# A tuned two-layer graph-attention kernel: first rows on two queues, right weights loaded earlier, scaling, residual rows and bias work moved

## The chip, the cores and the metric

One core of one Trainium2 chip. The metric is the device time of one execution in microseconds (us), as the median of several runs.

The engines in the traces: PE is TensorE, DVE is VectorE, ACT is ScalarE, POOL is GpSimd, SP is SyncE. SPq and ACTq are the points where SyncE and ScalarE issue transfers. SBUF is the on-chip memory that holds tiles, PSUM the banks into which TensorE writes. X, Y, Z and V are four of these banks, and the products are named after them. An evacuation is the step of VectorE or ScalarE that reads a finished bank and so frees it. The granted clock is the share of TensorE's full clock that the trace records: 0.50 is half rate.

## The reference

128 graphs of 64 nodes with 768 features, float32. Two layers of attention between layer norms, the weights 768x768:

```python
h = maximum(layernorm(x), 0)
for l in range(2):
    m_left, m_right = h @ W_left[l].T, h @ W_right[l].T
    u_left  = einsum('bih,bjh->bij', h, m_left)  / sqrt(768)
    u_right = einsum('bih,bjh->bij', h, m_right) / sqrt(768)
    u = upper triangle with diagonal from u_left, the rest from u_right (with adj)
    e = exp(u) * adj
    att = e / (sum(e) + 1e-10)
    ctx = att @ (h @ W_lin[l].T + b_lin[l])
    h = relu(layer_norm(ctx, ln_a[l], ln_b[l]))
return x + h
```

## The kernel before

It works on 16 blocks of 512 rows. Each layer has two passes: the first projects each block with the left and right weights and makes the attention; the second makes the linear product, the context and the norm. Each product of a 768x768 weight uses a scheme of seven half-size products instead of eight, which needs four sums of weight quarters (`sums_w`) and four sums of token quarters (`sums_t`). These sums read their inputs from SBUF.

```python
def sums_w(l, kind, eng):            # four sums, 128x1152 each
    ...
    for o, f, a, b in (("S1", "tensor_add", "S3", "A22"), ("S2", "tensor_sub", "S1", "A11"), ...):
        queue.append(lambda ...: getattr(eng, f)(t[o], t[a], t[b]))

def sums_t(key, eng=nc.gpsimd):      # four sums, 128x768 each: T1, T2, T3, T4
    ...
    for o, m, n in (("T1", "B12", "B11"), ("T2", "B22", "T1"), ("T3", "B22", "B12"), ("T4", "B21", "T2")):
        queue.append(lambda ...: sub(o, m, n))
```

Work beside the matmuls is put in a queue, and one piece is taken from it after each product (`pump(1)`). The order of the program is the order on each engine; nothing is rescheduled. The start of the first pass:

```python
if (l, 0) not in XR:
    load_rows(l, 0, sp)                    # rows of block 0, by SyncE
load_adj(0)
if l == 0:
    load_w(0, "l")
    transpose_rows(0, 0, sp)               # layer norm of the rows, transposes, store of the block
    flush()
    sums_t((1, 0, 0), nc.vector)           # on VectorE for this block alone
    ...
    sums_w(0, "l", nc.vector)
    ...
    load_w(0, "r")                         # issued behind the store
    sums_w(0, "r", nc.gpsimd)
queue.append(lambda: masks(0))
flush()
load_rows(l, 1, sp)
```

After this start, each block's queue holds the next block's preparation, and ends with `masks(u)` (GpSimd, needs the adjacency) and `sums_t` (GpSimd, needs the block). The third and fourth token sum are held back to the last product groups (`late`). In the second block, the last weights' bias work, centring and sums are appended, ahead of `late`.

Of the kernel before, what the change touches and what calls it, by code (L numbers as in the profile page):

```python
# [10 lines left out]
F32 = mybir.dt.float32  # L11
# [6 lines left out]
def kernel(  # L18
# [103 lines left out]
             ("X", "A12", "B21"), ("Z", "S4", "B22"), ("V", "A22", "T4"))  # L122

    HT, TS = {}, {}

    def tokens_of(key):
        ht = HT[key]
# [30 lines left out]
    nc.gpsimd.memset(eps_in, EPS_IN)  # L158
    floor = const.tile([P, 1], F32, name="floor")
    nc.gpsimd.memset(floor, 1e-30)  # L160

    diff = const.tile([P, S], I32, name="diff")
    tri = const.tile([P, 2, S], F32, name="tri")
# [2 lines left out]
        nc.gpsimd.iota(diff[r], pattern=[[-1, S]], base=0, channel_multiplier=1)  # L166
    nc.vector.tensor_scalar(tri[:, 0, :], diff, 0.0, None, op0=ALU.is_le)
    nc.vector.tensor_scalar(tri[:, 1, :], diff, 0.0, None, op0=ALU.is_gt)
    a_col, b_col = column("a_col", ln_a[0]), column("b_col", ln_b[0])

    def mean_var(mv, halves):
        st = stat.tile([P, 2, 6], F32, name="st")
        for n in range(2):
# [3 lines left out]

    XR = {}

    def load_rows(l, u, pool):  # L180

        XR[l, u] = []
        for g in range(2):
            t = pool.tile([P, 2, H], F32, name="x", bufs=2)
            for a in range(4):
                i = 4 * g + a
                src = x[u * NBB + i] if l == 0 else ROWS[u][i]
                nc.sync.dma_start(t[a * 32:(a + 1) * 32], src.rearrange("(k j) h -> j k h", k=2))
            XR[l, u].extend([t[:, 0, :], t[:, 1, :]])

    def load_h(which, l, u):
# [3 lines left out]
    def affine(which, l, u, step=1):  # L195

        def part(c0):
            for c in range(c0, c0 + step):
                ht = HT[which, l, u][:, c, :]
                nc.scalar.activation(ht, ht, AF.Relu, bias=b_col[:, c:c + 1], scale=a_col[:, c:c + 1])  # L200

        for c in range(0, C if l else 0, step):
            queue.append(lambda c=c: part(c))

    def transpose_rows(l, u, pool):

        key, xr = (1, l, u), XR[l, u]
        if l == 0:
            mv = stat.tile([P, Q, 2], F32, name="mv0", bufs=2)
            sd = stat.tile([P, Q], F32, name="sd0", bufs=2)  # L210
            rs = stat.tile([P, Q], F32, name="rs0", bufs=2)
            nb = stat.tile([P, Q], F32, name="nb0", bufs=2)

            def scale(q0, q1):
                nc.scalar.activation(sd[:, q0:q1], mv[:, q0:q1, 1], AF.Sqrt, bias=eps_in)
                nc.vector.reciprocal(rs[:, q0:q1], sd[:, q0:q1])
                nc.vector.scalar_tensor_tensor(nb[:, q0:q1], mv[:, q0:q1, 0], -1.0, rs[:, q0:q1],
                                               op0=ALU.mult, op1=ALU.mult)

            def norm(q):  # L220
                nc.scalar.activation(xr[q], xr[q], AF.Relu, bias=nb[:, q:q + 1], scale=rs[:, q:q + 1])

            for q in range(Q):
                queue.append(lambda q=q: mean_var(mv[:, q, :], [xr[q][:, :HH], xr[q][:, HH:]]))
                if u == 0:
                    queue.append(lambda q=q: scale(q, q + 1))
                    queue.append(lambda q=q: norm(q))
            if u:
                queue.append(lambda: scale(0, Q))
                for q in range(Q):  # L230
                    queue.append(lambda q=q: norm(q))
        if (l, u) == (0, 0):

            ht = HT[key] = big.tile([P, C, T], F32, name="ht")

            def turn(c0):
                p = ps_aux.tile([P, 2, T], F32, name="aux")
                for c in range(2):
                    for q in range(Q):
                        nc.tensor.transpose(p[:, c, q * P:(q + 1) * P],  # L240
                                            xr[q][:, (c0 + c) * P:(c0 + c + 1) * P], ident)
                for c in range(2):
                    nc.scalar.copy(ht[:, c0 + c, :].rearrange("p (a q j) -> p q a j", a=4, q=Q),
                                   p[:, c].rearrange("p (q a j) -> p q a j", a=4, q=Q))

            for c in range(0, C, 2):
                queue.append(lambda c=c: turn(c))
            queue.append(lambda: nc.sync.dma_start(KEPT[l][u], ht))
            return

        xb = pool.tile([P, H // 32, Q, 32], F32, name="xb", bufs=1)

        def store():
            to = KEPT[l][u].rearrange("(b i) c t -> i c b t", b=4)
            for a in range(4):
                nc.sync.dma_start(to[:, :, :, a * P:(a + 1) * P],
                                  xb[a * 32:(a + 1) * 32].rearrange("i (c b) q j -> i c b (q j)", b=4))

        for q in range(Q):
            queue.append(lambda q=q: nc.vector.transpose(  # L260
                xb[:, :, q, :], xr[q].rearrange("p (b j) -> p b j", j=32)))
        queue.append(store)


    def pass_one(l, aside):
        with tc.tile_pool(name=f"one{l}", bufs=2, reuse_waits="tile") as sp:
# [107 lines left out]

                CHAIN[u] = chain()

            if (l, 0) not in XR:
                load_rows(l, 0, sp)
            load_adj(0)
            if l == 0:  # L380
                load_w(0, "l")
                transpose_rows(0, 0, sp)
                flush()

                sums_t((1, 0, 0), nc.vector)
                tokens = [queue.popleft() for _ in range(4)]
                sums_w(0, "l", nc.vector)
                sums = [queue.popleft() for _ in range(4)]
                queue.extend(sums[:2] + tokens[:2] + [sums[2], tokens[2], sums[3], tokens[3]])
                load_w(0, "r")  # L390
                sums_w(0, "r", nc.gpsimd)
            queue.append(lambda: masks(0))
            flush()
            load_rows(l, 1, sp)
            for u in range(NB):
                if u == 0:
                    queue.extend([lambda: None] * 7)
                if u + 1 < NB:
                    prepare(u + 1)
                else:  # L400
# [26 lines left out]
    def bias(l):  # L427

        row("b1", b_lin[l], 0, HH, big)
        row("b2", b_lin[l], HH, H, big)  # L430
        b1, b2 = rows["b1"], rows["b2"]
        bm = stat.tile([P, 2], F32, name="bm", bufs=1)

        def centred():
            nc.vector.reduce_sum(bm[:, 0:1], b1, axis=mybir.AxisListType.X)
            nc.vector.reduce_sum(bm[:, 1:2], b2, axis=mybir.AxisListType.X)
            nc.vector.tensor_add(bm[:, 0:1], bm[:, 0:1], bm[:, 1:2])
            nc.vector.tensor_scalar_mul(bm[:, 0:1], bm[:, 0:1], -1.0 / H)
            nc.gpsimd.tensor_sub(b2, b2, b1)
            nc.vector.tensor_scalar_add(b1, b1, bm[:, 0:1])  # L440

        queue.append(centred)


    def pass_two(l, aside):
        last = l == L - 1
        with tc.tile_pool(name=f"two{l}", bufs=2, reuse_waits="tile") as sp:
# [25 lines left out]
            def batch(r, k, h):  # L473
                return 4 * (h if k == 0 else 1 - h) + r + 2 * k

            def finish(u, r):
                cx = context(u, r)
                zs = [sp.tile([P, H], F32, name="z", bufs=2) for _ in range(2)]
                xs = []
                if last:  # L480
                    for k in range(2):
                        xr = sp.tile([P, H], F32, name="xr", bufs=2)
                        for h in range(PAIR):
                            nc.sync.dma_start(xr[h * S:(h + 1) * S], x[u * NBB + batch(r, k, h)])
                        xs.append(xr)
                two = "p (n d) -> p n d"
                ss = stat.tile([P, 2], F32, name="ss")
                sd = stat.tile([P, 2], F32, name="sd1")
# [7 lines left out]
                if last:  # L496
# [13 lines left out]
                    queue.append(lambda: None)  # L510
                    queue.append(lambda: done(0))
                    queue.append(lambda: done(1))
                    return

                def scaled(k):
# [49 lines left out]
            for u in range(NB):  # L565
                for r in range(2):
# [8 lines left out]
                    if r == 0:  # L575
                        if u + 1 < NB:
                            load(u + 1)
                            queue.extend(nop * 3)
                            affine(2, l, u + 1, 2)
                            if turn:  # L580
                                load_rows(1, 0, sp)
                        elif turn:
                            queue.append(lambda: load_h(1, 1, 0))
                            queue.extend(nop * 4)
                            affine(1, 1, 0, 3)
                        queue.extend(nop * (7 - len(queue)))
                        if u in aside:
                            loaded = aside[u]()
                    else:
                        if u + 1 < NB:  # L590
                            sums_t((2, l, u + 1))
                            if turn:
                                transpose_rows(1, 0, sp)
                        elif turn:
                            sums_t((1, 1, 0))
                        if u in aside:
                            loaded()
# [56 lines left out]
```

## Time and profile before

| | before |
|---|---|
| median of 3 runs, us | 2994.14 (2992.59 to 2994.21) |
| span of the profiled run, us | 2994.0 |
| TensorE busy | 2919.1 us, 97% |
| first projection starts at | 21.8 |
| second pass of layer 0 starts at | 1011.7 |
| first projection of layer 1 starts at | 1503.6 |
| second pass of layer 1 starts at | 2477.7 |
| last context ends at | 2979.9 |

The last five rows are from TensorE's timeline: four starts of matmul groups and the end of the last one. The lines of the profile that name the waits stand in the prediction.

### The profile page before, as it was taken

Reading aid. Unit: us, or ns where it says so; the run is one execution under the profiler, and the core shown is the slowest. Engines: PE = TensorE matmul, PEld = TensorE weight load, DVE = VectorE, ACT = ScalarE, POOL = GpSimd, SP = SyncE. Lnnn points to the kernel's source line nnn. Section 1 sums busy time; section 2 is a strip of 40 time slices with the busy share of each in tenths; the row PEclk is TensorE's granted clock in tenths of the full one; section 3 lists DMA queues with packets and bytes.
Section 4 is the critical chain, followed back from the end, with each engine's and each line's share of the span. In section 5 each row is a group of like instructions: output and inputs, shape, how many; then the busy total and the mean of one; then the engine's idle time right before and its main releaser. Section 6 shows DMA issues by size and latency. Waiting matters only on the chain.

```text
span 2994.0 us, 37473 instructions
## 1 busy us (share of the span) xinstructions
PE 2919.1 (97%) x14872; PEld 2248.1 (75%) x14872; DVE 1135.8 (38%) x2310; ACT 583.2 (19%) x1112; POOL 769.9 (26%) x484
## 2 busy tenths in 40 slices
PE   6899999999999999999998999999999999999998
PEld 5778888888888755555587888888888885555554
DVE  4344443343333232222323333333333324555665
ACT  2111211121111122222311111111111112222221
POOL 1131111111111153232213111111211113555564
PEclk9999999999999999999999999999999999999999
DMA  6422243224322243333443432243224203655554
GB/s 175 127 69 69 75 112 88 69 74 114 88 69 70 77 146 122 99 115 105 134 108 107 113 93 69 70 111 95 69 69 111 74 24 113 174 152 150 164 148 133
DMA packets 228719, 310.23 MB, mean 104 GB/s; under 512 B 53696, under 2 KB 179136, under 8 KB 220352
## 3 DMA queue, kind: packets, MB, share of 16 engines
q1 hardware_dynamic: 228544, 307.84, 37.5%
q8 instruction: 117, 1.92, 0.3%
q14 instruction: 58, 0.48, 0.1%
HBM read 202.91 MB, written 104.86 MB: 103 GB/s over the span
## 4 chain that ended last, share of the span: by engine, by line
PE 89%; DMA 4%; POOL 2%; DVE 2%; SPq 1%; ACT 1%; issue 1%; DVEq 0%; POOLq 0%; ACTq 0%
PE Z L309 15%; PE V L309 15%; PE X L309 15%; PE Z L535 8%; PE Y L309 8%; PE V L535 7%; PE X L535 7%; PE aux L343 5%; PE Y L535 4%; PE aux L469 3%; DMA x<-in_x_dram 1%; DMA xr<-in_x_dram 1%; POOL ts L140 1%; DMA h<-xb 1%; POOL w_n_S L118 1%
## 5 line engine op out<-in xcount | busy, mean ns | idle before, releaser
L279 POOL TENSOR_TENSOR wm<-adj,tri 128x256 f32<-128x256 f32 x64 | 45.1, 726 | 1393.9 <-DMA adj<-in_adj_dram 1306.0
L140 POOL TENSOR_TENSOR ts<-ht 128x768 f32<-128x768 f32 x126 | 243.7, 1934 | 289.4 <-PE Y L309 156.1
L309 PE MATMUL V<-ts,w_l_A 128*128 128x256 f32 x1152 | 282.0, 381 | 4.3 <-POOL ts L140 3.7
L309 PE MATMUL V<-ts,w_r_A 128*128 128x256 f32 x1152 | 280.8, 380 | 0.6 <-DVE n L330 0.6
L309 PE MATMUL X<-ht,w_l_A 128*128 128x256 f32 x1152 | 280.8, 380 | 0.0
L309 PE MATMUL X<-ht,w_r_A 128*128 128x256 f32 x1152 | 280.0, 379 | 0.0
L535 PE MATMUL X<-w_n_A,ht 128*128 128x384 f32 x768 | 268.8, 486 | 0.0
L535 PE MATMUL V<-w_n_A,ts 128*128 128x384 f32 x768 | 268.7, 486 | 0.0
L328 ACT COPY n<-X 128x256 f32<-128x256 f32 x192 | 71.5, 373 | 993.2 <-PE X L309 993.2
L330 DVE TENSOR_TENSOR n<-V,u 128x256 f32<-128x256 f32 x384 | 161.9, 422 | 243.6 <-PE V L309 243.1
L309 PEld LDWEIGHTS V<-ts,w_l_A 128*128 128x128 f32 x1152 | 219.8, 191 | 35.6 <-POOL ts L140 4.5
L309 PEld LDWEIGHTS V<-ts,w_r_A 128*128 128x128 f32 x1152 | 219.2, 191 | 31.9 <-DVE n L330 2.1
L309 PEld LDWEIGHTS X<-ht,w_l_A 128*128 128x128 f32 x1152 | 219.4, 191 | 30.6 <-issue 0.6
L309 PEld LDWEIGHTS X<-ht,w_r_A 128*128 128x128 f32 x1152 | 218.9, 190 | 29.8
L140 POOL TENSOR_TENSOR ts<-ht,ts 128x768 f32<-128x768 f32 x126 | 239.0, 1897 | 4.6 <-issue 2.1
L535 PEld LDWEIGHTS V<-w_n_A,ts 128*128 128x128 f32 x768 | 146.2, 190 | 102.3 <-issue 0.9
L535 PEld LDWEIGHTS X<-w_n_A,ht 128*128 128x128 f32 x768 | 145.8, 190 | 101.6 <-issue 0.3
L491 ACT ACTIVATE z<-aux 128x768 f32<-128x768 f32 x128 | 102.5, 806 | 607.1 <-PE aux L469 607.1
L323 DVE TENSOR_TENSOR u<-Y,s 128x256 f32<-128x256 f32 x192 | 81.4, 424 | 360.4 <-PE Y L309 353.9
L330 DVE TENSOR_TENSOR n<-Z,u 128x256 f32<-128x256 f32 x192 | 81.3, 424 | 305.0 <-PE Z L309 304.9
L326 DVE TENSOR_TENSOR u<-Z,u 128x256 f32<-128x256 f32 x192 | 81.4, 424 | 284.2 <-PE Z L309 283.8
L545 POOL TENSOR_TENSOR u2b<-u,b 128x384 f32<-128x384 f32 x64 | 63.8, 997 | 476.6 <-DVE u L543 463.1
(101 smaller groups left out, 4029.4 us busy)
## 6 DMA issues: line engine op xcount, KB each, us to landing
ht<-h SPq DMA_DIRECT2D x63, 1536.0 KB, 7.4
h<-xb SPq DMA_DIRECT2D x124, 384.0 KB, 5.8
x<-in_x_dram SPq DMA_DIRECT2D x128, 192.0 KB, 8.5
z<-z SPq DMA_DIRECT2D x128, 192.0 KB, 3.0
x<-z SPq DMA_DIRECT2D x128, 192.0 KB, 8.6
xr<-in_x_dram SPq DMA_DIRECT2D x128, 192.0 KB, 4.1
out_dram<-xr SPq DMA_DIRECT2D x128, 192.0 KB, 2.7
adj<-in_adj_dram SPq DMA_DIRECT2D x64, 128.0 KB, 2.8
```

Of the source, the lines that this page charges most:

```text
L140: eng.tensor_sub(b[o], b[m], b[n])
L279: nc.gpsimd.tensor_tensor(WM[u][:, :, k], ADJ[u][:, :, 1 - k], t, op=ALU.mult)
L309: nc.tensor.matmul(p, w[a][:, c, g * P:(g + 1) * P], b[t][:, c, :], start=(new and c == 0), stop=(c == CH - 1), skip_group_check=True)
L323: nc.vector.tensor_add(u2, p, s1)
L326: nc.vector.tensor_add(u4, p, u2)
L328: nc.scalar.copy(to, pb)
L330: nc.vector.tensor_add(to, pb, (u4 if i == 3 else u2).rearrange("p (b s) -> p b s", s=S))
L343: nc.tensor.matmul(p[h * S:(h + 1) * S, q, :], ht[:, c, b * S:(b + 1) * S], m[c // CH][:, c % CH, b].rearrange("p k j -> p (k j)"), start= ...
L469: nc.tensor.matmul(cx[k][i, m, :HH], at[j, q, :], hl[j, q, m * HH:(m + 1) * HH], start=True, stop=True)
L491: nc.scalar.activation(zs[k].rearrange(two, n=2), cx[k], AF.Square, accum_out=ss[:, k:k + 1])
L535: nc.tensor.matmul(p, b[t][:, c, r * P:(r + 1) * P], w[a][:, c, :], start=(new and c == 0), stop=(c == CH - 1), skip_group_check=True)
L545: nc.gpsimd.tensor_add(u2b, u2, rows["b2"])
```

## The change

Its intent is to take TensorE's named waits away: at the start, in the first block, at the bias work of both layers, at the scaling on both borders, and where the residual rows had not landed. The core of the diff (cut: a helper that only gathers closures, and the two columns of the norm, which load later and are passed on as `cols`):

```diff
@@ start
+    warm = const.tile([P, 1], F32, name="warm")
+    nc.scalar.activation(warm, eps_in, AF.Sqrt)
...
-                nc.sync.dma_start(t[a * 32:(a + 1) * 32], src.rearrange("(k j) h -> j k h", k=2))
+                engines[a % 2].dma_start(t[a * 32:(a + 1) * 32], src.rearrange("(k j) h -> j k h", k=2))
...
+                queue.append(stats[0])
                 for q in range(Q):
-                    queue.append(lambda q=q: norm(q))
+                    queue.extend(stats[q + 1:q + 2] + [scales[q], norms[q]])
...
-            if (l, 0) not in XR:
-                load_rows(l, 0, sp)
-            load_adj(0)
             if l == 0:
+                load_rows(0, 0, sp, (nc.sync, nc.scalar))
                 load_w(0, "l")
+                load_w(0, "r")
                 transpose_rows(0, 0, sp)
                 flush()
...
-                load_w(0, "r")
                 sums_w(0, "r", nc.gpsimd)
+            load_adj(0)
...
-                    queue.extend([lambda: None] * 7)
+                    queue.extend([lambda: None] * 9)
@@ bias
-            nc.gpsimd.tensor_sub(b2, b2, b1)
+            nc.vector.tensor_sub(b2, b2, b1)
@@ residual rows
+                if last and not u and not r:
+                    residual(u, r)
+                xs = XS.get((u, r))
...
+                    if u < NB - 1 or r == 0:
+                        queue.append(lambda: residual(u + r, 1 - r))
@@ scaling at the borders
                             load(u + 1)
-                            queue.extend(nop * 3)
-                            affine(2, l, u + 1, 2)
+                            if u:
+                                queue.extend(nop * 4)
+                                affine(2, l, u + 1, 2)
...
                             queue.append(lambda: load_h(1, 1, 0))
-                            queue.extend(nop * 4)
-                            affine(1, 1, 0, 3)
...
                         if u + 1 < NB:
+                            if u == 0:
+                                affine(2, l, 1, 2)
                             sums_t((2, l, u + 1))
...
                         elif turn:
+                            affine(1, 1, 0, 2)
                             sums_t((1, 1, 0))
```

More of the change, by code (lines that the diff above doesn't have):

```diff
@@ L124 @@
     HT, TS = {}, {}
+    cols = []
     def tokens_of(key):
@@ L168 @@
     nc.vector.tensor_scalar(tri[:, 1, :], diff, 0.0, None, op0=ALU.is_gt)
-    a_col, b_col = column("a_col", ln_a[0]), column("b_col", ln_b[0])
     def mean_var(mv, halves):
@@ L178, with load_rows @@
     XR = {}
-    def load_rows(l, u, pool):
+    def load_rows(l, u, pool, engines=(nc.sync, nc.sync)):
         XR[l, u] = []
@@ L199, in part @@
                 ht = HT[which, l, u][:, c, :]
-                nc.scalar.activation(ht, ht, AF.Relu, bias=b_col[:, c:c + 1], scale=a_col[:, c:c + 1])
+                nc.scalar.activation(ht, ht, AF.Relu, bias=cols[1][:, c:c + 1], scale=cols[0][:, c:c + 1])
         for c in range(0, C if l else 0, step):
@@ L221, in norm @@
                 nc.scalar.activation(xr[q], xr[q], AF.Relu, bias=nb[:, q:q + 1], scale=rs[:, q:q + 1])
-            for q in range(Q):
-                queue.append(lambda q=q: mean_var(mv[:, q, :], [xr[q][:, :HH], xr[q][:, HH:]]))
-                if u == 0:
-                    queue.append(lambda q=q: scale(q, q + 1))
-                    queue.append(lambda q=q: norm(q))
+            stats = [lambda q=q: mean_var(mv[:, q, :], [xr[q][:, :HH], xr[q][:, HH:]]) for q in range(Q)]
+            norms = [lambda q=q: norm(q) for q in range(Q)]
             if u:
-                queue.append(lambda: scale(0, Q))
+                queue.extend(stats + [lambda: scale(0, Q)] + norms)
+            else:
+                scales = [lambda q=q: scale(q, q + 1) for q in range(Q)]
+                queue.append(stats[0])
                 for q in range(Q):
-                    queue.append(lambda q=q: norm(q))
+                    queue.extend(stats[q + 1:q + 2] + [scales[q], norms[q]])
         if (l, u) == (0, 0):
@@ L394, in pass_one @@
             load_rows(l, 1, sp)
+            if l == 0:
+                cols.extend([column("a_col", ln_a[0]), column("b_col", ln_b[0])])
             for u in range(NB):
                 if u == 0:
-                    queue.extend([lambda: None] * 7)
+                    queue.extend([lambda: None] * 9)
                 if u + 1 < NB:
@@ L474, in batch, with residual @@
                 return 4 * (h if k == 0 else 1 - h) + r + 2 * k
+            XS = {}
+            def residual(u, r):
+                XS[u, r] = [sp.tile([P, H], F32, name="xr", bufs=2) for _ in range(2)]
+                for k in range(2):
+                    for h in range(PAIR):
+                        nc.sync.dma_start(XS[u, r][k][h * S:(h + 1) * S], x[u * NBB + batch(r, k, h)])
             def finish(u, r):
@@ L478, in finish @@
                 zs = [sp.tile([P, H], F32, name="z", bufs=2) for _ in range(2)]
-                xs = []
-                if last:
-                    for k in range(2):
-                        xr = sp.tile([P, H], F32, name="xr", bufs=2)
-                        for h in range(PAIR):
-                            nc.sync.dma_start(xr[h * S:(h + 1) * S], x[u * NBB + batch(r, k, h)])
-                        xs.append(xr)
+                if last and not u and not r:
+                    residual(u, r)
+                xs = XS.get((u, r))
                 two = "p (n d) -> p n d"
```

## The prediction

> **What bounds the kernel now.** I read the page first, then the waits of TensorE, then the timelines of all engines around each wait. The page says what the limit is:
>
> ```profile
> PE 2919.1 (97%) x14872; PEld 2248.1 (75%) x14872; DVE 1135.8 (38%) x2310; ACT 583.2 (19%) x1112; POOL 769.9 (26%) x484
> ...
> PE 89%; DMA 4%; POOL 2%; DVE 2%; SPq 1%; ACT 1%; issue 1%; DVEq 0%; POOLq 0%; ACTq 0%
> ```
>
> TensorE is busy 97% of the span, and 89% of the chain that ended last is matmuls. The change touches no matmul: in the built program TensorE's list is the same, row for row. So only the time in which TensorE does not run at its pace can be won. That pace can be read from the chain's recurring pieces. In the first pass over the blocks the score matmuls come every 59.98 us (229.25, 289.23, ...). In the second, the Y products come every 15.19 us, twice a block. Two layers of 16 blocks at this pace need 32 x 59.98 + 32 x 30.38 = 2891.5 us. Of the 102.5 us above it, 21.8 lie before the first projection and 14.1 after the last matmul. Some 66 us are losses between. The waits of TensorE name them:
>
> ```profile
> PE Z L309 <- DVE u L326: 17.5, 4, 8.9
> PE Z L535 <- DVE u L548: 7.9, 2, 5.0
> PE Z L309 <- DVE n L330: 6.9, 1, 6.9
> PE V L309 <- POOL ts L140: 3.7, 2, 3.4
> PE Y L309 <- POOL ts L140: 2.6, 1, 2.6
> PE aux L469 <- DVE n L556: 2.4, 2, 1.2
> ```
>
> Columns: total us, number of waits, longest. The direct waits come to some 44 us. Most of the rest is half speed after them: in the granted clock 42 to 48 us stands at 0.50. The engine named is rarely the cause. In the timelines it was itself held, as in these three pairs:
>
> ```profile
> 41.01 1.02 DVE L174 BATCH_NORM_STATS2 st<-x 128x6 f32<-128x384 f32 x2 [8.37 <-DMA x<-in_x_dram]
> 44.08 2.93 PE L309 MATMUL Z<-ht,w_l_S 128*128 128x256 f32 x6 [5.42 <-DVE u L326]
> 1617.10 0.42 DVE L440 TENSOR_SCALAR b<-b,bm 128x384 f32<-128x384 f32 x1 [9.89 <-POOL b L439]
> 1617.91 2.93 PE L309 MATMUL Z<-ht,w_r_S 128*128 128x256 f32 x6 [8.85 <-DVE u L326]
> 2498.82 4.33 ACT L200 ACTIVATE ht<-ht,b_col,a_col 128x512 f32<-128x512 f32 x6 [19.30 <-DMA ht<-h]
> 2508.97 3.90 PE L535 MATMUL Z<-w_n_S,ht 128*128 128x384 f32 x6 [5.00 <-DVE u L548]
> ```
>
> First column start, second duration, in brackets the idle time before and what ended it. VectorE stands at statistics whose rows have not landed, or at one small bias step behind GpSimd; ScalarE stands at a scaling whose block has not landed. All three run in order, so the evacuations that free TensorE's banks stand behind that.
>
> **What the Trainium skill says.** "TensorE: Matmul & The Clock Gate", section "What's actually happening": after an idle window of about 3.4 us the array falls to half rate, and needs about 3.4 us of work to rise. The trace agrees: after waits of 2.6 us and more a first group of six takes 2.6 to 2.9 us for 1.46, and I count 1.4 to 2.1 us lost for each. "DMA: Bandwidth & Descriptors", section "Issuing engines are not separate DMA queues": a second issuing engine saves only issue time. Eight row issues took 3.84 us at the start, while rows came at 217 to 244 GB/s until 10 us, so I expect little there. "ScalarE: Activation LUTs", section "What ACT_TABLE_LOAD costs": about 1283 ns; the trace has 1.28 us at 9.11 us. "GPSIMD Engine Reference", section 3.1: a two-input add there is 1.96 times VectorE's; here a 128x1152 step takes 2.62 us on GpSimd and 1.36 on VectorE.
>
> **The change, part by part.**
>
> Start. The table load (1.28) leaves the path, and each statistic goes ahead of the previous rows' scaling. Before, the four row tiles follow each other by 1.95 us: stats 1.02, aggregate 0.21, root 0.29, two small steps 0.36. After, the period is ScalarE's 1.03 + 0.30 plus the small steps 0.36, some 1.7. But ScalarE issues its half only after its table load, and in the built program its pieces of the second tile wait for earlier transfers. I take the first statistic at 7.7 as now and the second tile 1 us late: the last scaling ends at 17.1 for 17.94. Gain 0.8; first projection at 20.9.
>
> First block. The right weights now load in the 6 us (18 to 23.5) in which the DMA moved nothing. The next rows then land at about 33 to 36 us, for 41, and their statistics stand two products later. The stall of 5.42 and the 2.1 of slow clock go. But the later parts move too: the store of transposed rows comes after product 21 instead of 19, at 20.9 + 0.9 + 21 x 1.295 plus two transposes = 51.4 (before 58.16). From that store to TensorE's Y product of block 1 runs a chain of transfers and GpSimd work (store 10.4, block and rows 8.8, adjacency 6.6, masks and two sums 5.1): 31.0 us, from 58.16 to 89.17. So Y comes at 82.4, where TensorE is ready at some 77. The gain there is 6.7 with the start's 0.8, and the wait at Y grows from 2.6 to some 5.
>
> Bias, layer 0. The subtraction on VectorE costs 0.55 and no longer waits 10.85. TensorE's 6.95 and most of the 1.85 go. But block 2 needs its third sum, which stands on GpSimd behind four centrings and four weight sums:
>
> ```profile
> 143.40 1.40 POOL L279 TENSOR_TENSOR wm<-adj,tri 128x256 f32<-128x256 f32 x2 [50.75 <-DMA adj<-in_adj_dram]
> 148.40 0.99 POOL L439 TENSOR_TENSOR b<-b,b 128x384 f32<-128x384 f32 x1
> 153.17 4.17 POOL L110 TENSOR_TENSOR w_n_A<-w_n_A,wm 128x1152 f32<-128x1152 f32 x2 [3.78 <-DVE wm L106]
> 172.35 1.80 POOL L140 TENSOR_TENSOR ts<-ht 128x768 f32<-128x768 f32 x1
> 174.20 2.58 PE L309 MATMUL V<-ts,w_l_A 128*128 128x256 f32 x6 [3.39 <-POOL ts L140]
> ```
>
> This queue starts with the adjacency's landing, which only shifts, and loses 0.99 + 3.78 + 0.30 = 5.1. So V comes 6.4 (the shift, less slower clock) + 5.1 = 11.5 earlier, after a wait of some 10 us; a little more half clock leaves **11.2 for the start, first block and bias of layer 0 together**.
>
> Bias, layer 1. The 8.85, 0.32 and 2 of clock go, but VectorE's means still cost TensorE some 1.8, and in the same GpSimd queue the third sum ends at 1641.9 - 5.1 = 1636.8 on the old clock face, where V started at 1641.9. Less 1.9 of half clock after the new wait of 5: **3.1**.
>
> Scaling at the borders. Between the layers it moves half a block later, behind the squares. The 2.89 goes, with 1.8 and 0.9 of slow clock in products and context: 5.6. The row transposes two products later save 1.42 + 0.58 at 1520, less 0.3: **7.3**. Into the last pass the 5.00 goes, with 1.8 + 0.9 of clock: 7.8 with small gaps. The sums of block 1 come later (second one at 2509.2, by squares, roots, three scalings and two additions in GpSimd's order) but TensorE needs it at 2511.1: **7.8**.
>
> Residual rows a step ahead. VectorE no longer waits for them:
>
> ```profile
> 2683.55 0.96 DVE L504 SCALAR_TENSOR_TENSOR xr<-z,xr 128x768 f32<-128x768 f32 x1 [3.27 <-DMA xr<-in_x_dram]
> 2687.53 1.51 PE L469 MATMUL aux<-n,at 64*64 64x384 f32 x14 [1.24 <-DVE n L556]
> ```
>
> The Y products stand 17.28 us apart there for 15.19, twice, and five other steps lose 0.1 to 0.5. I take **4.5** of 5.3. At the end the rows were not waited for (the last sums wait for GpSimd), so the tail stays.
>
> Sum: 11.2 + 3.1 + 7.3 + 7.8 + 4.5 = 33.9 us, so 2994.1 - 33.9 = 2960.2 us.
>
> **Rivals.** (1) Everything adds up: all waits and slow clock between the first projection and the tail go, some 60 us, to 2934. For it: each named holder is attacked. Against: GpSimd's queue at both bias places and the transfer chain into block 1 stand behind the waits removed. (2) The loads run against each other at the start: the left weights share with ScalarE's row pieces, whose second half is issued late; the first projection comes at 22 to 24 and the whole first stage with it, 2962 to 2964. (3) The residual rows now stand in SyncE's queue ahead of the next block, and wait for the output to leave the same buffers. I put the block some 3 us later; ScalarE's scaling (4.3 us) then ends after the squares could begin. TensorE has about 3 us of slack there. If not, up to 1 us in each of 14 blocks returns, 2970 to 2975. (4) The late sums at the two borders miss by 2 to 4 us each: 2964 to 2968.
>
> **Range and chances.** Rival 1 in part (GpSimd quicker, rows earlier) sets the low end, 2952; rivals 2 to 4, one or two in part, the high end, 2970. Over 2% needs 2934 or less, more than all stalls here less the two queues: 1%. Slower by 2% has no mechanism: 1%.
>
> **What would show it.** In the changed profile: no wait of VectorE at statistics near 41, none at the bias; TensorE waits some 5 us at Y near 82 and 10 at V near 152 to 163, and 5 near block 2 of layer 1, all put down to GpSimd's sums; no wait of TensorE at the two scalings; second-pass steps at 15.19 throughout. It is wrong if the waits of TensorE sum to under 15 us after the start (rival 1), if the first projection comes after 21.8, or if ScalarE's scaling waits for blocks in the last pass show up as TensorE gaps.

## The result

| | before | after |
|---|---|---|
| median, us (4 runs each) | 2993.36 (2989.72 to 2994.21) | 2972.26 (2971.97 to 2973.10) |
| ratio | | 0.9932 (95%: 0.9915 to 0.9949), the same within 2% |

A ratio is the mean time of one kernel's fast runs over that of the other's of the same rounds, so it is not quite the ratio of the medians quoted. The gain is 21.1 us between the medians. The prediction said 2960.2, with 2952 to 2970: the measured time lies 2.3 us above its range.

The stages show where the gain is missing. Each row is the length of a stage in the profiled runs, from the starts of matmul groups; the gains sum to 23.8, the difference of the two profiled spans (2994.0 and 2970.2).

| stage | before | after | gained | predicted |
|---|---|---|---|---|
| to the second pass of layer 0 | 1011.7 | 1013.5 | -1.8 | 11.2 |
| from there to the first projection of layer 1 | 491.9 | 487.3 | 4.6 | 5.6 |
| first pass of layer 1 | 974.2 | 967.8 | 6.4 | 4.8 |
| second pass of layer 1, to its last context | 502.2 | 487.6 | 14.6 | 12.3 |
| tail | 14.1 | 14.0 | 0.1 | 0 |

(The predicted 7.3 at the first border is split: its 1.7 at the row transposes falls into the first pass of layer 1, beside the 3.1 of its bias work.) All stages but the first gained 25.7, for 22.7 predicted. The first should have won 11.2 and lost 1.8. **The shortfall is in the first stage alone.**

The page of the changed kernel, engine shares and the chain that ended last:

```profile
PE 2910.5 (98%) x14872; PEld 2246.1 (76%) x14872; DVE 1130.0 (38%) x2312; ACT 582.6 (20%) x1113; POOL 768.2 (26%) x482
...
PE 93%; DMA 3%; POOL 2%; SPq 1%; DVE 1%; issue 0%; ACT 0%; DVEq 0%; POOLq 0%; ACTq 0%
```

TensorE has the same 14872 matmuls and is busy 8.6 us less. That fits fewer matmuls at half clock after a wait (the mean granted clock went from 0.991 or 0.992 to 0.993), but was not added up group by group. Its waits in the changed kernel (total us, number, longest; the three smallest kinds are cut):

```profile
PE V L310 <- POOL ts L141: 11.2, 2, 9.0
PE aux L241 <- DMA x<-in_x_dram: 11.1, 1, 11.1
PE aux L241 <- ACT x L222: 7.7, 3, 5.4
PE Y L310 <- POOL ts L141: 5.1, 1, 5.1
PE V L310 <- DVE ts L141: 4.1, 1, 4.1
PE Y L310 <- DVE ts L141: 2.9, 1, 2.9
```

The fourth and the 9.0 in the first were predicted (5 us at Y, 10 at V); the other 2.2 of the first, in layer 1, was predicted as 5. The third is longer than before (there 4.3 in three waits). In the last two TensorE waits for VectorE's token sums of the first block: the one at V is new, the one at Y was 0.9 before. VectorE's timeline of the changed kernel there (start, duration, instruction, in brackets the idle time before):

```profile
25.39 3.00 DVE L141 TENSOR_TENSOR ts<-ht,ts 128x768 f32<-128x768 f32 x1 [0.28 <-ACT ht L244]
28.32 3.77 DVE L118 TENSOR_TENSOR w_l_A<-w_l_A,w_l_A 128x1152 f32<-128x1152 f32 x1
32.01 3.36 DVE L141 TENSOR_TENSOR ts<-ht 128x768 f32<-128x768 f32 x1
```

and the second and third of these in the kernel before:

```profile
24.01 1.35 DVE L118 TENSOR_TENSOR w_l_A<-w_l_A,w_l_A 128x1152 f32<-128x1152 f32 x1
25.28 0.95 DVE L140 TENSOR_TENSOR ts<-ht 128x768 f32<-128x768 f32 x1
```

They stand back to back, so nothing waited between them: the instructions themselves last three times as long. What is new beside them is GpSimd's work, in the changed kernel (two of its four sums of the right weights):

```profile
27.54 3.33 POOL L118 TENSOR_TENSOR w_r_A<-w_r_A,w_r_A 128x1152 f32<-128x1152 f32 x1
30.84 3.72 POOL L118 TENSOR_TENSOR w_r_S<-w_r_A,w_r_S 128x1152 f32<-128x1152 f32 x1
```

In the kernel before, these sums ran from 34.15, with 2.62 us each, when VectorE's sums had been done since 28.4:

```profile
34.15 2.62 POOL L118 TENSOR_TENSOR w_r_S<-w_r_A,w_r_A 128x1152 f32<-128x1152 f32 x1 [32.41 <-DMA w_r_A<-in_w_right_dram]
```

Now the right weights land by 20.9. The third of the stretched sums makes the tokens of the product V. It ends at 35.37, just before V starts:

```profile
35.42 2.93 PE L310 MATMUL V<-ts,w_l_A 128*128 128x256 f32 x6 [4.11 <-DVE ts L141]
```

2.93 us for six matmuls that take 1.46 at full rate: the clock was granted at 0.50 from 34 to 40 us.

The first projection is late too, at 24.09 for 21.78 before and 20.9 predicted. VectorE stood at the statistics of the second row tile, while ScalarE's second pair of row pieces had been issued only between 4.53 and 8.23 us. VectorE's timeline, then ScalarE's:

```profile
14.36 1.02 DVE L175 BATCH_NORM_STATS2 st<-x 128x6 f32<-128x384 f32 x2 [4.42 <-DMA x<-in_x_dram]
```

```profile
4.53 3.70 ACTq L189 DMA_DIRECT2D x<-in_x_dram  x2
```

So there are two theories, and they can both hold. **A**: ScalarE's pieces of the second row tile come late behind the weights, 3 us at the first projection. **B**: GpSimd's two-input work holds VectorE's two-input work up, some 8 us. Rivals: the transfers now running at that time slow VectorE; or the early load of the right weights was never worth anything.

### The profile page after: what moved, and what is told of

The parts are those of the page before. It is cut to its first block, busy times and chain, and to the rows that moved or that the text cites. A ratio compares the mean times of both kernels' runs of the same rounds, so it can differ in the third digit from the quotient of the medians.

```text
span 2970.2 us, 37457 instructions
## 1 busy us (share of the span) xinstructions
PE 2910.5 (98%) x14872; PEld 2246.1 (76%) x14872; DVE 1130.0 (38%) x2312; ACT 582.6 (20%) x1113; POOL 768.2 (26%) x482
## 4 chain that ended last, share of the span: by engine, by line
PE 93%; DMA 3%; POOL 2%; SPq 1%; DVE 1%; issue 0%; ACT 0%; DVEq 0%; POOLq 0%; ACTq 0%
PE V L310 16%; PE Z L310 16%; PE X L310 16%; PE Z L543 8%; PE V L543 8%; PE X L543 8%; PE Y L310 8%; PE aux L344 5%; PE Y L543 5%; PE aux L471 3%; DMA x<-in_x_dram 1%; DMA h<-xb 1%; POOL w_n_A L110 1%; POOL w_n_S L118 1%; POOL ts L141 0%; DMA adj<-in_adj_dram 0%
## 5 line engine op out<-in xcount | busy, mean ns | idle before, releaser
L310 PE MATMUL V<-ts,w_l_A 128*128 128x256 f32 x1152 | 284.4, 383 | 15.3 <-POOL ts L141 11.2
```

The lines of the kernel that those rows point to most:

```text
L310: nc.tensor.matmul(p, w[a][:, c, g * P:(g + 1) * P], b[t][:, c, :], start=(new and c == 0), stop=(c == CH - 1), skip_group_check=True)
```

## The experiments

The kernel before ran beside each (medians 2992.6 to 2993.3). Line 140 of the kernel before (the token sums) is line 141 of the changed one.

### Rows by one queue (e1)

```diff
-                load_rows(0, 0, sp, (nc.sync, nc.scalar))
+                load_rows(0, 0, sp)
```

> The changed kernel with the first block's rows issued by SyncE alone again. Theory A (ScalarE's row pieces come late): the second row tile lands near 10 us instead of 14.3, VectorE's statistics of it no longer wait 4.4 us for rows, and the first projection comes at 20.5 to 21.5 us instead of 24.1. Theory B (GpSimd's sums of the right weights stretch VectorE's two-input sums) says that this collision stays: VectorE's token and weight sums still take 1.5 to 3.8 us each and TensorE still waits some 3 us at the first Y and 4 us at the first V, so that 1 to 3 us of 2972.3 are won and no more (2969 to 2971). Rival C (the late first projection is all that failed, the rest only follows it): the whole 13 us come back, near 2960. Rival D (the second queue is of use, and the row tile is late because the chip's memory is slow there): the first projection comes at 24 or later, time unchanged or worse.

Measured: 2971.07 us (2970.77 to 2971.67), ratio 0.9926. First projection at 20.70. VectorE's wait for the second tile:

```profile
10.66 1.02 DVE L175 BATCH_NORM_STATS2 st<-x 128x6 f32<-128x384 f32 x2 [1.10 <-DMA x<-in_x_dram]
```

Theory A is right for the start: with one queue the tile's statistics start 3.7 us earlier, and the first projection comes at 20.7 where the prediction wanted 20.9. In the six profiled runs with two queues it comes at 24.1 to 25.7, in the five with one at 20.4 to 20.7. The early right weights are not what delays the tile: in e3 below they load late, and its statistics still start at 14.13. Whether the late issue or the sharing with the left weights does it was not separated. The waits of 2.86 at Y and 4.11 at V stay, so rival C falls. Only 1.2 us of the 3.4 reach the end: 2.6 are still there at the second pass of layer 0 (1010.87), and 1.8 go again in the first pass of layer 1, where TensorE waits 2.69 and 3.26 us at V for 2.18 and 2.17. Of the 0.51 at the first of these, 0.40 is one 128x3 step of VectorE that met GpSimd's masks (0.69 us for 0.29). Why the second differs from run to run of nearly the same code stays open.

### Sums of the right weights on VectorE (e2)

```diff
-                sums_w(0, "r", nc.gpsimd)
+                kept = list(queue); queue.clear()
+                sums_w(0, "r", nc.vector)
+                right = list(queue); queue.clear()
+                queue.extend(kept)
...
-                    queue.extend([lambda: None] * 9)
+                    queue.extend([lambda: None] * 5 + right if l == 0 else [lambda: None] * 9)
```

> The changed kernel with the four sums of the right weights moved from GpSimd to VectorE, four products later; every transfer is issued as before, so the DMA traffic at 20 to 38 us is the same. Theory B (contention of GpSimd with VectorE): the L141 token sums fall back to 0.96 to 1.2 us from 3.0 and 3.4, the L118 weight sums to 1.36 from 3.8 and 1.9; TensorE's waits of 2.9 us at the first Y and 4.1 us at the first V go, with some 2 us of half clock; the first projection stays at 24.1; Y of the second block comes near 86 to 87 instead of 95.0; the time falls by 7 to 9 us, to 2963 to 2965. Rival (the transfers of the right weights or of later loads slow VectorE's reads of memory): the stretches stay, the time stays at 2972 or grows by a part of 5.5 us, since VectorE has four sums more.

Measured: 2963.62 us (2962.88 to 2964.68), ratio 0.9901. VectorE's sums beside the same transfers, but with GpSimd idle:

```profile
26.86 1.35 DVE L118 TENSOR_TENSOR w_l_A<-w_l_A,w_l_A 128x1152 f32<-128x1152 f32 x1
28.12 0.95 DVE L141 TENSOR_TENSOR ts<-ht 128x768 f32<-128x768 f32 x1
```

The durations are those of the kernel before, to the hundredth, and the time falls by 8.6 us. Y of the second block starts at 86.55, for 95.01. VectorE has more work than in the changed kernel, and the kernel is faster.

### Right weights loaded late again (e3)

```diff
                 load_w(0, "l")
-                load_w(0, "r")
                 transpose_rows(0, 0, sp)
...
+                load_w(0, "r")
                 sums_w(0, "r", nc.gpsimd)
```

> The changed kernel with the load of the right weights put back behind the store of the first block, where the kernel before has it; everything else stays. Theory B: GpSimd's sums then start near 35 us, after VectorE's, so the stretches of VectorE's sums are gone (0.96 to 1.4 us each) and with them the waits at the first Y and V; but the next block's rows land at about 41 us again, VectorE stands there at statistics and TensorE waits some 5 us near 44, with 2 us of half clock. The two should cancel to within 3 us: 2969 to 2975. If the early load cost nothing (rival), the time grows by some 7 us, to 2979.

Measured: 2971.78 us (2969.35 to 2972.49), ratio 0.9927. GpSimd's sums start at 37.32 and VectorE's take 0.95 and 1.35 again, with no wait at the first V. But VectorE stands at the next block's statistics, and TensorE waits 3.68 at 46.39:

```profile
44.79 1.02 DVE L175 BATCH_NORM_STATS2 st<-x 128x6 f32<-128x384 f32 x2 [5.50 <-DMA x<-in_x_dram]
```

The early load does win about what the prediction gave it (5.42 and 2.1 us of slow clock): e2 and e3 are both free of the collision, and e2, which loads early, is 8.2 us faster, although VectorE also makes the right weights' sums there. In the changed kernel the collision costs as much. The two cancel.

### The collision alone, in the kernel before (e4 and e8)

```diff
 e4:
+                for i in range(12):                       # 128x384 each, result unused
+                    nc.gpsimd.tensor_sub(spare, b["B12"][:, :, half], b["B11"][:, :, half])
 e8:
+                nc.gpsimd.tensor_sub(spare[:, :, :TH], b["B12"], b["B11"])
+                for _ in range(4):                        # 128x1152 each, result unused
+                    nc.gpsimd.tensor_sub(spare, wl["A12"], wl["A22"])
```

> The kernel before with twelve GpSimd subtractions of 128x384 added whose result nobody reads; they take the first block as soon as ScalarE has written it, near 22 us, and so run for some 12 us beside VectorE's first sums. No transfer is added or moved. Theory B (GpSimd's two-input work holds up VectorE's two-input work on the same chip memory): VectorE's L140 token sums of 128x768 go from 0.95 to 2 to 3.4 us and its L118 weight sums of 128x1152 from 1.35 to 2 to 3.8, GpSimd's own take more than half of the 1.8 us that a 128x768 one takes alone, and TensorE waits 3 to 5 us at its first Y and V where the kernel before waits 0.91 and nothing; VectorE's sums out of PSUM stay at 0.42. Rival (transfers, or the changed order, stretch VectorE): the durations stay at 0.95 and 1.35 and TensorE's waits as they are.

Measured, one look: VectorE's sums are stretched, with no transfer changed. VectorE's timeline in e4, then GpSimd's:

```profile
25.32 2.15 DVE L118 TENSOR_TENSOR w_l_A<-w_l_A,w_l_A 128x1152 f32<-128x1152 f32 x1
27.39 1.75 DVE L140 TENSOR_TENSOR ts<-ht 128x768 f32<-128x768 f32 x1
```

```profile
21.81 17.30 POOL L388 TENSOR_TENSOR spare<-ht 128x384 f32<-128x384 f32 x12 [20.06 <-ACT ht L243]
```

Theory B is confirmed in its direction and missed in its size: 1.75 and 2.15, not up to 3.4 and 3.8, and TensorE waits 1.40 at Y and 0.88 at V. VectorE's sums out of PSUM stayed at 0.42, as expected. Both kinds of sum are longer by the same 0.80 us (1.75 less 0.95, 2.15 less 1.35), although one is half as large again as the other. A subtraction of this size takes GpSimd 0.99 us alone (the bias line shown in the prediction). So the loss looks like the length of one GpSimd instruction, and e8 tests that with larger ones.

> The kernel before with one GpSimd subtraction of 128x768 and four of 128x1152 whose result nobody reads, the size of the right weights' sums, from some 22 us on, beside VectorE's first sums; no transfer added or moved. The twelve small ones stretched VectorE's sums from 0.95 to 1.75 and from 1.35 to 2.15, less than in the changed kernel (up to 3.4 and 3.8). If the size of GpSimd's instruction sets how long VectorE stands (it can go on only between two of them, or seldom within one), the stretches are as in the changed kernel, 3 us and more, and TensorE waits 3 and 4 us at Y and V. If they stay at 1.75 and 2.15, the rest of the changed kernel's stretch is from something else (transfers of the right weights, which tiles are read), and stays open.

Measured, one look, VectorE's timeline in e8, then GpSimd's:

```profile
25.28 3.77 DVE L118 TENSOR_TENSOR w_l_A<-w_l_A,w_l_A 128x1152 f32<-128x1152 f32 x1
28.97 3.36 DVE L140 TENSOR_TENSOR ts<-ht 128x768 f32<-128x768 f32 x1
```

```profile
24.62 13.87 POOL L394 TENSOR_TENSOR w_r_S<-w_l_A,w_l_A 128x1152 f32<-128x1152 f32 x4
```

3.77 and 3.36 are the very durations of the changed kernel, made in the kernel before by nothing but GpSimd's instructions; no transfer was moved. The loss is 2.42 and 2.41 us for GpSimd instructions that take 2.62 alone. TensorE's waits come too: 4.12 at V as expected, 3.29 after, but only 1.43 at Y, where 3 were expected. VectorE waits out about one whole GpSimd instruction before each of its own two-input sums; the size of GpSimd's instruction sets the loss.

### Both faults of the start mended (e5)

The edits of e1 and e2 together.

> Both edits together: rows by SyncE alone, the right weights' sums on VectorE. If theories A and B together are the whole of the shortfall at the start: first projection at 20.5 to 21.5 us, no wait of TensorE over 1 us before 80 us, second pass of the first layer from about 1001 to 1003 us instead of 1013.5, time 2960 to 2962, what the prediction had. If the chain of transfers behind the first block's store sets when the second block starts, whatever TensorE does before it: a longer wait at Y of the second block takes up the gain, and the time stays over 2966.

Measured: 2960.15 us (2958.55 to 2961.94), ratio 0.9890. First projection at 20.70, Y of the second block at 83.04 after a wait of 5.32, V at 162.83 after 9.03, second pass of layer 0 at 1001.63. The prediction had 20.9, 82.4 with some 5, 152 to 163 with some 10, and 2960.2. With A and B mended its sum holds.

### The other parts, each undone alone in the changed kernel (u1, u2, u3)

```diff
 u1:
-            nc.vector.tensor_sub(b2, b2, b1)
+            nc.gpsimd.tensor_sub(b2, b2, b1)
 u2: the hunk "scaling at the borders" undone
 u3:
-                if last and not u and not r:
+                if last:
                     residual(u, r)
...
-                    if u < NB - 1 or r == 0:
-                        queue.append(lambda: residual(u + r, 1 - r))
```

> The changed kernel with the bias subtraction alone back on GpSimd. If it is worth what the kernel before lost there, VectorE waits for GpSimd at L440's addition again in both layers, and TensorE some 7 us near 150 and some 9 us near 1608. But after each of these TensorE waits for GpSimd's third sum anyway (9.0 and 2.2 us in the changed kernel), and that wait shrinks when TensorE comes late: so the time grows not by 16 us but by what GpSimd's queue grows, the subtraction (1.0), its wait for VectorE's means (3.8) and the slow clock: 3 to 7 us a layer, together 6 to 12, 2978 to 2984. If the waits simply add (rival), 2988.

> The changed kernel with the scaling of the blocks at the two layer borders alone put back to its earlier step. TensorE's waits of 2.9 us at Z near 1493 and of 5.0 near 2500 come back with 1.5 to 3 us of half clock each, and the row transposes at the first border come two products earlier (waits of 1.4 and 0.6 us). Worth 7.3 and 7.8 us in the prediction, but the changed kernel won 4.6 at the first border up to the first projection of layer 1; so 10 to 15 us, 2982 to 2987. Rival: the wait for the block's landing moves into another wait, and under 5 us come back.

> The changed kernel with the residual rows alone loaded in their own step again. The prediction's term is 4.5 us, with two waits of TensorE of 1.2 us near 2660 to 2700 and Y products 17.3 us apart instead of 15.2; so 2975 to 2978. Rival: the waits there were chance, or a result of the border before; then the time stays within 1 us of 2972.

| | median, us | over the changed kernel | in its own stages (profiled runs) | predicted worth |
|---|---|---|---|---|
| u1, bias | 2981.32 (2980.30 to 2982.52) | +9.1 | layer 0: 4.6, layer 1: 3.5 | 5.1 and 3.1 |
| u2, scaling | 2986.14 (2984.08 to 2988.62) | +13.9 | first border 4.3, last pass 8.7 | 7.3 and 7.8 |
| u3, residual rows | 2974.56 (2972.86 to 2977.27) | +2.3 | last pass 1.9 | 4.5 |

The profiled run of u2 was its slowest (its first projection came at 25.71), that of u3 its fastest, and u3's lowest time lies among those of the changed kernel.

u1 brings TensorE's waits of 7.16 and 8.50 us back and lets the later 9.0 at V shrink to 3.40: taking a wait away only moved it, as the prediction had it, and the part is worth the 8 to 9 us that GpSimd's queue gets shorter. u2 brings 2.78 and 5.65 us at Z back. u3 fell under its expectation: VectorE waits for residual rows 13 times again, 14.8 us in all, but the longest is 1.8 (before 3.3), and no wait of TensorE appears. By the medians the residual rows alone were worth about half of what was predicted. In the last pass u2 and u3 make 10.6 of the 14.6 us. The other 4 stand in the same steps: behind the border, the Y products of the last pass exceed their distance of 15.19 us by 6.4 in all in the kernel before (the prediction counted 5.3), by nothing in the changed one, and by 1.9 in u3. Why late rows cost 6.4 in one profiled run and 1.9 in the other stays open.

### Beyond both kernels (e6, e7, e9)

With the start mended, the waits left are those for GpSimd's sums. e6 puts the masks behind the first two token sums, so that these need not stand behind the adjacency:

```diff
-                queue.append(lambda: masks(u))
                 sums_t((1, l, u))
+                queue.insert(len(queue) - 2, lambda: masks(u))
```

> The kernel of the run before with rows by SyncE alone and the right weights' sums on VectorE (2960.2 us), and the masks of each block put behind its first two token sums on GpSimd instead of ahead of them. GpSimd's sums of the second block then need only the block, not the adjacency, which lands later. If the masks' wait for the adjacency is what holds Y of the second block (5.3 us at 83), that wait goes with 1.4 us of half clock, and GpSimd's queue in the next block is some 3 us shorter when the adjacency lands: 2950 to 2954. If the block itself lands as late as the adjacency, under 2 us are won. If the later wait of 9.0 us for GpSimd's third sum takes the gain back: 2958 to 2960.

Measured: 2942.40 us (2941.55 to 2943.44), ratio 0.9831. More than expected. GpSimd in e6, at the second block:

```profile
68.36 1.81 POOL L141 TENSOR_TENSOR ts<-ht 128x768 f32<-128x768 f32 x1 [36.60 <-DMA ht<-h]
70.25 1.81 POOL L141 TENSOR_TENSOR ts<-ht,ts 128x768 f32<-128x768 f32 x1
76.81 1.41 POOL L280 TENSOR_TENSOR wm<-adj,tri 128x256 f32<-128x256 f32 x2 [4.75 <-DMA adj<-in_adj_dram]
```

The sums are done at 72.1, where e5 started them at 79.3 behind the adjacency; TensorE's wait at Y is gone. I had counted the shorter queue (some 3 us) for the later wait of 9.0, but not that the adjacency of the next block lands earlier too (130.4 for 137.2): that wait fell to 0.51. A new one of 3.42 came at 136.8. There VectorE's 128x3 steps of the weight means, 0.16 us alone, took 1.94 and 2.04 beside GpSimd's centrings, and its evacuations stood behind them:

```profile
131.92 1.94 DVE L105 TENSOR_TENSOR wm<-wm 128x3 f32<-128x3 f32 x1
133.89 2.04 DVE L106 TENSOR_SCALAR wm<-wm 128x3 f32<-128x3 f32 x1
```

The second multiplies one tile by a constant, so a step need not have two inputs to be held up.

e7 also puts the last weights' centrings and sums behind the fourth token sum on GpSimd, and spreads VectorE's bias and mean steps over six products (cut: the lines that split these steps and gather them):

```diff
-                            queue.extend([lambda: None] * 3 + late)
+                            queue.extend([lambda: None] * 3 + late + behind)   # behind: centrings and sums
...
-                queue.extend([lambda: None] * 6)
+                queue.extend([GAP] * 6)            # filled with VectorE's bias and mean steps
```

> The run before it and one more: in both layers GpSimd does the third and fourth token sum of block 2 ahead of the last weights' four centrings and four sums, and VectorE's means of these weights are spread over six products. The waits of 9.0 us at V near 163 and of 2.1 near 1619 should go, with 1.5 us of half clock each, and most of the 2.4 us at V near 1595: some 16 us under the run before it, 2935 to 2940, with hardly a wait of TensorE over 1 us left after the start. If the weights' sums, now beside VectorE's work of the next block, hold up its evacuations or the next block's first sums, a new wait near 180 to 220 takes a part back: over 2943.

Measured: 2952.07 us (2950.04 to 2953.72), ratio 0.9863: slower than e6. In layer 0 it did what was wanted (second pass at 981.07, for 988.39), but in layer 1 VectorE came to the bias before its rows had landed, and TensorE waited 17.0 us:

```profile
1566.96 0.55 DVE L448 TENSOR_REDUCE bm<-b 128x1 f32<-128x384 f32 x1 [19.98 <-DMA b<-in_b_lin_dram]
```

That was my mistake: I had checked the order, but not when the weights land in layer 1. e9 keeps VectorE's steps at their old place in layer 1:

```diff
-            queue.extend(items.pop(0) if q is GAP else q for q in kept)
+            queue.extend(items.pop(0) if q is GAP and not l else q for q in kept)
+            queue.extend(items)
```

> The run before it with its one fault mended: in layer 1 VectorE's bias and weight means go back behind the first token sums (there the weights land late, and VectorE stood 20 us at the bias rows), GpSimd's centrings and sums still behind the third and fourth token sum. By stages: layer 0 up to its second pass as in the run before it, 981 us; from there to the second pass of layer 1 as in the run that had only the masks moved, 1450 us, less up to 2 us for the wait of 0.7 and the half speed of VectorE's small steps beside GpSimd. So 2942.4 less 7.3, less up to 2: 2933 to 2936. If the weights' sums behind T4 reach into the next stage in layer 1: 2937 and more.

Measured: 2933.46 us (2932.04 to 2936.85), ratio 0.9804 (0.9790 to 0.9818), as expected and 38.8 us under the changed kernel; whether it is 2% under the kernel before is unclear by this interval. The first of TensorE's waits in e9, the start's:

```profile
PE aux L246 <- ACT x L227: 14.7, 4, 10.5
```

All others together come to 1.9 us (0.9, 0.7 and 0.3).

## Why the prediction was wrong

**What held.** The bound, and the pace outside the stalls: TensorE's list was unchanged and only waits and half clock were won. The store-to-Y chain of 31.0 us was right: 31.3 in the changed kernel (63.69 to 95.01), 31.6 in e5. The waits at Y (5.1) and at V (9.0) came as named, put down to GpSimd's sums, though some 12 us later than named; the one in layer 1 came as 2.2 for 5. The bias held: predicted 5.1 in layer 0 and 3.1 in layer 1, measured 4.6 and 3.5. No wait came back at the borders, and rival 3 did not show: no TensorE gaps in the last pass.

**Which step failed.** "First block. The right weights now load in the 6 us (18 to 23.5) in which the DMA moved nothing." The step asked what the earlier load does to the DMA queue and to the rows behind it; that part was right, as e2 beside e3 shows. It did not ask what the weights' landing sets off. GpSimd's four sums stood ready for these weights, and moved from 34 to 21 us, beside VectorE's first sums. The prediction had the store at 51.4; it came at 63.69. Of these 12.3 us, 3.2 are the later first projection, 6.1 the waits of 2.9 and 4.1 (less the 0.9 that the prediction allowed at Y), and 2.6 the half clock in the two groups from V on; 0.4 is left over. e2 wins 8.6 us back by moving the GpSimd work alone, and e8 makes the same durations by adding such work alone. The cause is shown.

The Trainium skill states it: "SBUF — State Buffer", section "Who interferes with whom", says that a VectorE instruction with two SBUF inputs contends with a GpSimd instruction that reads SBUF. Its section "SBUF: two separate sides" adds that whichever of the two starts first has the shared ports for its whole instruction while the other waits. The runs agree: 0.80 us lost to GpSimd instructions of 0.99, 2.41 to those of 2.62; nothing lost by sums out of PSUM (0.42). I had looked up what a GpSimd addition costs, not what it does to VectorE. The trace before held the hint, in the last pass, where one addition of VectorE stands beside a token sum of GpSimd (2559.75 to 2561.84) and the one before it had begun first:

```profile
2559.21 0.96 DVE L504 SCALAR_TENSOR_TENSOR xr<-z,xr 128x768 f32<-128x768 f32 x1 [1.00 <-DMA xr<-in_x_dram]
2560.55 2.11 DVE L504 SCALAR_TENSOR_TENSOR xr<-z,xr 128x768 f32<-128x768 f32 x1
```

The prediction showed a line of the first kind and took its duration as fixed.

**Which term was mis-sized.** "I take the first statistic at 7.7 as now and the second tile 1 us late." The statistics came 4.4 us after VectorE was free, and the first projection at 24.1, beyond the 21.8 that the prediction named as its own refutation. Rival 2 had this (22 to 24, and 2962 to 2964); its size was right, and alone it would have stayed in the range: e2, where only this fault is left, measured 2963.62. e1 shows that one queue gives 20.7.

**What the sum hid.** The border to layer 1 gave 4.6 for 5.6, and the residual rows 2 for 4.5 when undone alone (from few and scattered runs); the row transposes and the last pass gave more than their terms. These cancelled, and the total beyond the first stage was 25.7 for 22.7. e5's 2960.15 against 2960.2 is therefore partly luck: its first stage gained 10.1 for 11.2, with these errors cancelling behind it.

## What to carry to other kernels

When a load is moved earlier, follow what its landing releases: work of an idle engine that starts sooner can take the shared memory path of the engine you are waiting for, and each of that engine's two-input instructions then lasts longer by about one whole instruction of the other. Put such sums of GpSimd where VectorE reads PSUM or where nobody waits for VectorE; small GpSimd instructions hurt less than large ones. When a wait behind an in-order queue is removed, look at what that queue does next: the 17.8 us from e5 to e6 came from the order of GpSimd's queue alone.

## What the Trainium skill lacked or had wrong

- The page on SBUF named above is right in kind, but gives no example of two queues that both have work. The runs show that they take turns: of e4's twelve GpSimd subtractions, those beside VectorE's sums took 1.59 and 1.99 us in turn (1.00 once VectorE's sums were over), in e8 the four large ones 3.2 and 3.6 in turn (2.62 alone), while VectorE lost 0.80 and 2.41 per instruction. Which engine issued first at the start did not keep the other out.
- No page that I read gives a figure for a tiny VectorE step: it pays as much. 128x3 steps of 0.16 us, one with two inputs and one with a single input, took 1.94 and 2.04 beside GpSimd's centrings of 128x1152.
- No page that I read warns that a second issuing engine can make loads later: with ScalarE issuing half of the first rows, the second tile's statistics started at 14.36, with SyncE alone at 10.66.
- "TensorE: Matmul & The Clock Gate", section "What's actually happening", gives one idle window of about 3.4 us for half rate. In the changed kernel a wait of 2.17 us at 1631 was followed by six matmuls in 2.93 us, and one of 2.90 at 28 by six in 1.56: the length of the single wait doesn't tell. The prediction's "The trace agrees" was too strong for the same reason: in the kernel before, waits of 2.61 and 2.89 us, shorter than that window, were also followed by half rate.
